# Attention maxima in a two-layer kernel: combining two halves by a pairwise reduce

## The chip, the cores and the metric

The kernel runs on one core of a Trainium2 chip. The metric is the device time of one execution in microseconds, the median of several runs. One further execution was taken by the hardware profiler; its rows are what is called the profile or the trace here. TensorE (PE) does matmuls and transposes, VectorE (DVE), ScalarE (ACT) and GpSimd (POOL) work on elements, and SyncE (SP) issues most transfers. SBUF is the on-chip memory that all engines read; PSUM is the one that TensorE writes.

## The reference

Two layers are computed on an input of 2 x 1024 tokens of width 256. Layer 0 is an attention of 16 query heads on 8 key/value heads of size 16, multiplied by a feed-forward network whose weights are looked up in a table of 16 values. Layer 1 is a recurrence over time, multiplied by a mixture of 8 experts with 2 chosen per token. Only the attention matters for the change:

```python
scores = jnp.einsum('bsdkg,btdk->bkgst', q, k) / jnp.sqrt(jnp.float32(E))
w = jax.nn.softmax(scores, axis=-1)
ctx = jnp.einsum('bkgst,btdk->bkgsd', w, v)
```

The softmax runs over 1024 keys. The kernel subtracts each query's largest score before it takes the exponential, and it is this largest score that the changed line finishes.

## The kernel before

**The work.** A sequence of 1024 tokens and four of its heads (`T`) make a group; there are 2 x 4 = 8 groups. For each group the kernel makes three passes of small matmuls.

- `largest` (letter `m`, L309 and L316) multiplies 128 queries of one head with 512 keys (`mx`, 128x512 in PSUM) and VectorE reduces each row to its maximum, one column of the tile `top`. A block of 128 queries (`c`) needs eight of these: four heads (`i`) times two halves of the keys (`half`). `top` is therefore 128 x 2 x 4: partitions are queries, then the half, then the head. When the eighth is there, L320 takes the larger of the two halves for each head and writes it to slot 16 (`HD`) of the query tile `qn`. That slot meets a constant -1 in the key tile, so that the next product has the maximum subtracted already. Four buffers of `top` rotate.
- `turn_q` with `qTb` (letter `l`, L287) transposes `qn`, now with the maxima, for the second product.
- `weigh` (letter `w`, L340, and L332 in the first group) computes the scores with keys on partitions (`sc`), and ScalarE takes their exponential (`e`, L344). `gather` (letter `v`, L368 and L357) multiplies the exponentials with the values into `cx`; the sum of the weights comes along in a further column. `divide` (letter `y`) divides by it.

The matmuls of `largest` and `weigh` have 32 rows of contraction and take one of four row groups of TensorE each, so four can run side by side. Each writes a bank of its own; there are eight banks, given out in rotation (`bank`), and a matmul waits until the bank's last reader is through: L316 on VectorE for an `mx`, L344 on ScalarE for an `sc`.

**What runs beside it.** GpSimd turns the coded weights of the feed-forward network into numbers (`decode`, letter `z`): for each of 8 pieces and 16 table values it compares the codes with the value's number (L270, 128x544, integers to `pick`) and adds the result to the table of weights (L274, `wlut` plus `pick`, two operands in SBUF). It also rotates queries and keys (L241, L244). The feed-forward network of the tokens that are done (L559, L575) begins within the attention.

**The order.** There is no scheduler: the string `ORDER` is walked letter by letter, and each letter issues the next step of its kind. Every engine executes its instructions in the order in which they were issued, and waits at semaphores for the others. L320 has no letter of its own; it is issued within the step `m` that completes a block, right behind that step's L316, and the next instruction of VectorE is mostly the L316 of the next `mx`.

Of the kernel before, what the change touches and what calls it, by code (L numbers as in the profile page):

```python
# [15 lines left out]
ALU = mybir.AluOpType  # L16
AX = mybir.AxisListType
# [15 lines left out]
HD = 16  # L33
# [69 lines left out]
def attention(  # L103
# [11 lines left out]
    def bank(name):  # L115
        return singles[0].tile([P, 512], F32, tag="one", name=name)
# [18 lines left out]
    qns, kTs, vpf = [], [], []  # L135
# [164 lines left out]
    def largest(n, i):  # L300

        g, u = divmod(n, 16)
        b, T = divmod(g, NQT)
        c, half = divmod(u, 2)
        if (g, c) not in tops:
            tops[g, c] = att2.tile([P, 2, 4], F32, tag="top", name=f"top_{g}_{c}", bufs=4)
        at = slice(SLOT * i, SLOT * (i + 1))
        ps = bank(f"mx_{n}_{i}")
        nc.tensor.matmul(  # L309
            ps,  # L310
            qTs["qTa", g, c // BC][at, ts(c % BC, P)],
            kTs[b][at, T // 2, ts(half, 512)],
            start=True,
            stop=True,
        )
        nc.vector.tensor_reduce(tops[g, c][:, half, i : i + 1], ps, AX.X, ALU.max)  # L316
        done[g, c] = done.get((g, c), 0) + 1
        if done[g, c] == 8:
            top = tops.pop((g, c))
            nc.vector.tensor_tensor(qns[b][:, T, c, :, HD], top[:, 0, :], top[:, 1, :], ALU.max)  # L320

    def weigh(n, i):

# [91 lines left out]
    def each(f, *ranges):  # L415
# [10 lines left out]
        "j": each(turn_q, ["qTa"], range(GROUPS), range(2)),  # L426
        "l": each(turn_first, range(BC)) + each(turn_q, ["qTb"], range(GROUPS), range(2))[1:],
        "m": each(largest, range(UNITS), range(4)),
        "w": each(weigh, range(UNITS), (0, 2, 1, 3)),
        "v": each(gather, range(UNITS)),  # L430
# [1103 lines left out]
```

## Time and profile before

| | |
|---|---|
| median of 3 runs | 979.56 us (979.51 to 980.02) |
| the profiled execution's own time | 980.91 us |
| its span | 979.0 us |
| TensorE clock granted | 0.994 |
| the reduces L316 | 512, 324.7 us, 683 ns each |
| the exponentials L344 | 512, of 605 ns |
| the matmuls `mx` L309 | 1024 records (two for each of 512), 626 ns each |
| the matmuls `sc` L340 | 960 records (two for each of 480), 625 ns each |
| decode L270 to `pick`, L274 | 120 each; 2102 and 1337 ns |
| first and last L320 | 34.1 and 509.1 us |

The span is the time between the first and the last instruction in the profile; the execution's own time contains what lies around it. The page gives busy time by engine, then rows of 40 slices of the span in which a digit is the busy share in tenths, then the chain of work that ended last, followed back from the end, as shares of the span, then groups of instructions by line of the kernel. In a group, `out<-in` names what is written and read, with partitions x elements; after the count come busy time, mean ns of one, and the idle time of the engine just before them with what ended it. The view of waits lists, for an engine and a line, what the wait ended with, its total, how often, and the longest. The timeline gives single instructions, or runs of equal ones, with start and duration in us.

### The profile page before, as it was taken

To read this page: it belongs to the slowest core of one execution; us is meant where nothing else is said; L and a number is where in the kernel's file an instruction comes from. 1 tells how busy PE (TensorE), PEld (TensorE's weight loads), DVE (VectorE), ACT (ScalarE), POOL (GpSimd) and SP (SyncE) were. 2 spreads that over 40 slices of the span, in tenths; PEclk is the share of its full clock that TensorE was granted. 3 is DMA by queue.
4 is the path that set the end of the run, shared out by engine and by line. 5 is a ranking of instruction groups with operands and counts; after the bars stand their busy time and mean duration, and the time that the engine had idled before them with its cause. 6 is when DMAs were issued, how large, how long until landed. Compare 5 with 4: busy or idle time off the path is not lost.

```text
span 979.0 us, 17252 instructions
## 1 busy us (share of the span) xinstructions
PE 953.0 (97%) x6716; PEld 522.4 (53%) x6716; DVE 627.9 (64%) x1228; ACT 533.8 (55%) x1009; POOL 586.7 (60%) x485
## 2 busy tenths in 40 slices
PE   8999999999999999999999999999999999999974
PEld 4685433343333443443435475755457677777763
DVE  5898887887767767765760134466877635721993
ACT  4545856566675675766767545527323544464221
POOL 7999999999999999999902020202002355453243
PEclk9999999999999999999999999999999999999998
DMA  5000000000000000000000031003501122221232
GB/s 175 2 2 13 1 12 1 1 12 1 12 2 1 12 1 13 1 1 1 1 1 1 1 122 40 24 1 101 164 1 33 50 66 63 68 76 50 77 119 87
DMA packets 17864, 34.53 MB, mean 35 GB/s; under 512 B 2893, under 2 KB 11231, under 8 KB 17439
## 3 DMA queue, kind: packets, MB, share of 16 engines
q1 hardware_dynamic: 13527, 21.96, 7.1%
q0 software_dynamic: 3968, 10.80, 3.6%
q8 instruction: 54, 0.88, 0.4%
q10 hardware_dynamic: 288, 0.66, 0.2%
q14 instruction: 27, 0.22, 0.1%
HBM read 22.01 MB, written 11.40 MB: 34 GB/s over the span
## 4 chain that ended last, share of the span: by engine, by line
PE 91%; DVE 5%; issue 1%; DMA 1%; POOL 1%; ACT 0%; POOLq 0%; SPq 0%; ACTq 0%; DVEq 0%
PE sc L340 15%; PE mx L309 14%; PE cx L368 12%; PE gu L559 7%; PE gue L990 5%; PE d L575 4%; PE gus L750 4%; PE dne L1018 3%; PE qkv L218 3%; PE lev L1228 3%; PE sc L332 2%; PE rp L1132 1%; PE so L410 1%; PE vp L1159 1%; PE kp L1132 1%; PE ap L1132 1%
## 5 line engine op out<-in xcount | busy, mean ns | idle before, releaser
L316 DVE TENSOR_REDUCE top<-mx 128x1 f32<-128x512 f32 x512 | 324.7, 683 | 92.7 <-PE mx L309 61.7
L344 ACT ACTIVATE e<-sc 128x512 f32<-128x512 f32 x512 | 271.9, 605 | 139.3 <-PE sc L340 65.4
L309 PE MATMUL mx<-kT,qTa 32*128 32x512 f32 x1024 | 287.0, 626 | 0.4 <-DVE top L316 0.4
L270 POOL TENSOR_SCALAR pick<-idx,lut 128x544 f32<-128x544 int32 x120 | 252.3, 2102 | 11.3
L340 PE MATMUL sc<-qTb,kT 32*128 32x512 f32 x960 | 257.5, 625 | 0.5 <-DVE top L316 0.5
L274 POOL TENSOR_TENSOR wlut<-wlut,pick 128x544 f32<-128x544 f32 x120 | 160.4, 1337 | 10.0
L309 PEld LDWEIGHTS mx<-kT,qTa 32*128 32x128 f32 x1024 | 102.5, 183 | 66.1 <-DVE top L316 27.3
L340 PEld LDWEIGHTS sc<-qTb,kT 32*128 32x128 f32 x960 | 93.2, 183 | 79.3 <-DVE top L316 26.4
L368 PE MATMUL cx<-e,vpad 128*32 128x512 f32 x960 | 123.9, 603 | 0.0
L585 POOL TENSOR_TENSOR sgt<-s_sb,g 128x256 f32<-128x256 f32 x16 | 11.6, 728 | 161.1 <-ACT g L583 161.1
L963 POOL DMA_INDIRECT xg<-xn_h,who x39 | 39.4, 1009 | 94.8 <-PE s L1351 70.2
L1031 POOL DMA_INDIRECT y_h<-ye,who x39 | 39.9, 1024 | 69.2 <-ACT ye L1026 25.4
L559 PE MATMUL gu<-xnT,wlut 128*128 128x512 f32 x160 | 72.8, 597 | 0.0
L368 PEld LDWEIGHTS cx<-e,vpad 128*32 128x32 f32 x960 | 20.8, 108 | 84.2 <-issue 73.5
L1002 DVE TENSOR_TENSOR sge<-sge,gue 128x176 f32<-128x176 f32 x39 | 13.1, 338 | 73.4 <-ACT sge L1001 73.1
L569 DVE TENSOR_TENSOR h<-sg,gu 128x512 f32<-128x512 f32 x20 | 13.8, 688 | 65.4 <-ACT sg L568 50.3
L990 PE MATMUL gue<-wgu,xT 128*128 x156 | 53.0, 462 | 1.6 <-issue 1.0
L559 PEld LDWEIGHTS gu<-xnT,wlut 128*128 128x128 f32 x160 | 29.1, 190 | 34.0 <-issue 29.9
L575 PE MATMUL d<-wlut,h 128*128 128x256 f32 x192 | 44.1, 381 | 0.5 <-ACT s_sb L413 0.5
L750 PE MATMUL gus<-xnT,wgs 128*128 128x512 f32 (+1 forms) x96 | 43.1, 597 | 0.0
L1018 PE MATMUL dne<-wd,hTe 88*128 x156 | 40.0, 380 | 0.5 <-ACT hTe L1011 0.5
L575 PEld LDWEIGHTS d<-wlut,h 128*128 128x128 f32 x192 | 35.7, 190 | 8.1 <-issue 1.8
(235 smaller groups left out, 1346.6 us busy)
## 6 DMA issues: line engine op xcount, KB each, us to landing
xn_h<-xn SPq DMA_DIRECT2D x16, 256.0 KB, 3.4
yk<-y_h SPq DMA_DIRECT2D x16, 256.0 KB, 3.0
wgu<-in_wgu SPq DMA_DIRECT2D x1, 2816.0 KB, 10.9
idx<-in_idx SPq DMA_DIRECT2D x8, 272.0 KB, 2.7
out_x<-g SPq DMA_DIRECT2D x16, 128.0 KB, 1.7
wd<-in_wd SPq DMA_DIRECT2D x1, 1408.0 KB
xs<-in_x SPq DMA_DIRECT2D x2, 512.0 KB, 4.6
w<-in_w SPq DMA_DIRECT2D x1, 1024.0 KB
```

The costliest lines, as they stand in the source:

```text
L270: nc.gpsimd.tensor_scalar(dst, codes[piece], float(j), lut[:, j : j + 1], ALU.is_equal, ALU.mult)
L274: nc.gpsimd.tensor_tensor(wlut[:, at], wlut[:, at], dst, ALU.add)
L309: nc.tensor.matmul(ps, qTs["qTa", g, c // BC][at, ts(c % BC, P)], kTs[b][at, T // 2, ts(half, 512)], start=True, stop=True,)
L316: nc.vector.tensor_reduce(tops[g, c][:, half, i : i + 1], ps, AX.X, ALU.max)
L340: nc.tensor.matmul(ps, kTs[b][at, T // 2, ts(c, P)], qTs["qTb", g, h][at, :], start=True, stop=True)
L344: nc.scalar.activation(e, ps, AF.Exp, scale=1.0 / math.sqrt(E))
L368: nc.tensor.matmul(cxs[g, h][SLOT * i : SLOT * (i + 1), :], values(b, c, 4 * (T // 2) + i), es.pop((n, i)), start=(c == 0), stop=(c == CPB ...
L559: nc.tensor.matmul(hT0[which], wlut[:, lo + kc * P :][:, 0:P], xnT[:, kc, ts(n, 512)], start=(kc == 0), stop=(kc == KC - 1),)
L575: nc.tensor.matmul(po[:, 0:E], hidden(n)[:, f, ts(k, P)], wd0[:, f, :], start=(f == 0), stop=(f == NF0 - 1),)
L750: nc.tensor.matmul(ps[:sz, which, :], wgs[:, kc, which * SH_CH + lo : which * SH_CH + lo + sz], xnT[:, kc, ts(n, 512)], start=(kc == 0), s ...
L990: nc.tensor.matmul(ps[:, 0 : 2 * EI], xT[:, kc, :], late["gu"][:, kc, bass.ds(e * (2 * EI), 2 * EI)], start=(kc == 0), stop=(kc == KC - 1),)
L1018: nc.tensor.matmul(ps[:, 0:E], hT[:, k, :], late["d"][:, k, bass.ds(e * E, E)], start=(k == 0), stop=(k == 1),)
```

## The change

The eight maxima of a block are combined by `tensor_reduce` with `max` over a view of `top` whose innermost dimension is the half: for each of the four heads a pair of values that lie four elements apart. It reads one operand of 128x8 where the operation before read two of 128x4. The result goes to the same four places of `qn`.

```diff
         if done[g, c] == 8:
             top = tops.pop((g, c))
-            nc.vector.tensor_tensor(qns[b][:, T, c, :, HD], top[:, 0, :], top[:, 1, :], ALU.max)
+
+            nc.vector.tensor_reduce(
+                qns[b][:, T, c, :, HD], top.rearrange("p h i -> p i h"), AX.X, ALU.max
+            )
```

## The prediction

> **What bounds the kernel now.** I read the page's totals and chain first, then the groups with their shapes kept apart, then the changed line alone, then the timeline round single executions of it.
>
> ```profile
> PE 953.0 (97%) x6716; PEld 522.4 (53%) x6716; DVE 627.9 (64%) x1228; ACT 533.8 (55%) x1009; POOL 586.7 (60%) x485
> ...
> DVE 5898887887767767765760134466877635721993
> ...
> POOL 7999999999999999999902020202002355453243
> ...
> PE 91%; DVE 5%; issue 1%; DMA 1%; POOL 1%; ACT 0%; POOLq 0%; SPq 0%; ACTq 0%; DVEq 0%
> ```
>
> TensorE is on the chain for 91% of the span, VectorE for 5%. The changed line lies in the attention, the first 515 us (21 slices of 24.5 us); there VectorE is busy 60 to 90% and GpSimd nearly all the time, with the table decode of L270 and L274. So a saving on VectorE counts only where a matmul waits for it. The waits say that this happens:
>
> ```profile
> PEld mx L309 <- DVE top L316: 27.3, 59, 1.0
> PEld sc L340 <- DVE top L316: 26.4, 48, 1.0
> ```
>
> Columns: total us, times, longest. 53.7 us of weight loads wait for the reduce L316 to free a PSUM bank. TensorE hardly looks idle meanwhile, because these matmuls use 32 of 128 rows and four may run side by side: a late one spoils a group of four rather than stopping the engine.
>
> **The changed row** (groups by shape: count, then busy us and mean ns; idle):
>
> ```profile
> L320 DVE TENSOR_TENSOR qn<-top 128x4 f32<-128x4 f32 x64 | 26.0, 407 | 2.2
> ...
> L779 DVE TENSOR_REDUCE top<-left 128x4 f32<-128x32 f32 x4 | 0.7, 186 | 0.1
> ...
> L880 DVE TENSOR_REDUCE pos<-each 128x16 f32<-128x128 f32 x2 | 0.6, 286 | 0.1
> ```
>
> The line alone gives min/median/max of 166/168/1345 ns. A mean of 407 over a median of 168 on four elements is a tail. Listed one by one, 35 of the 64 last 166 to 170 ns (5.8 us together) and 29 are longer (20.2 us together; 15.3 us above 167 ns each). The timeline shows what the long ones share (start us, us):
>
> ```profile
> 454.72 1.33 POOL L274 TENSOR_TENSOR wlut<-wlut,pick 128x544 f32<-128x544 f32 x1
> 454.73 1.34 DVE L320 TENSOR_TENSOR qn<-top 128x4 f32<-128x4 f32 x1
> ```
>
> ```profile
> 107.30 2.10 POOL L270 TENSOR_SCALAR pick<-idx,lut 128x544 f32<-128x544 int32 x1
> 107.53 0.50 DVE L320 TENSOR_TENSOR qn<-top 128x4 f32<-128x4 f32 x1
> ```
>
> In the first pair both end together. Of the 29, 20 were issued behind a running L274 and every one ends 20 to 26 ns after it; they hold 13.0 us of the excess. The other nine came behind a young L270: eight end 729 to 733 ns after its start, one came so early that it ended at 197; 2.3 us. An L320 issued later into an L270 lasts 167 ns. So the operation of two SBUF operands waits while GpSimd reads SBUF.
>
> **Rule and row.** The Trainium skill, "SBUF — State Buffer", section "Who interferes with whom", states that a VectorE instruction with two SBUF inputs contends with a GpSimd instruction that reads SBUF, for the whole instruction, and that tensor_reduce never contends on trn2. "Whole" does not fit L270: the row is let go after 0.73 of 2.10 us. By the rule a random L320 would wait (2.10² + 1.34²)/(2 × 3.6) = 0.86 us in each L270/L274 period of about 3.6 us, 55 us over 64; measured are 15.3. I use 15.3. For the rule's other half there is a row, a one-input read of SBUF inside L274:
>
> ```profile
> 31.10 0.18 DVE L170 BATCH_NORM_AGGREGATE mv_a<-bst_a 128x2 f32<-128x6 f32 x1
> ```
>
> ```profile
> 30.92 1.33 POOL L274 TENSOR_TENSOR wlut<-wlut,pick 128x544 f32<-128x544 f32 x1
> ```
>
> With 1.15 us of L274 still to run it takes 0.18, like all 16 of its kind (181 to 184 ns). A rule against the change: "VectorE: DVE Perf Modes", section "Rules for kernel authors", calls tensor_reduce the slowest VectorE operation, to be expected at one element per cycle, and advises restructuring. By it, eight elements instead of four pairs cost four elements more: at L880 minus L779, (286 − 186)/96 = 1.04 ns each, 64 × 4 = 0.3 us. The rows decide below.
>
> **The change part by part.**
> - *Removed*: 64 L320 rows, 26.0 us of VectorE.
> - *Added*: 64 reduces 128x4<-128x8, in the same places with the same wait (on the last reduce into top). No row has this shape. The line through L779 and L880 gives 186 − 24 × 1.04 = 161 ns; L316 (512 elements, 683 ns, from PSUM) lies on it too (152.7 + 1.04 × 512 = 685), so outputs as such cost nothing visible. Bounds: 150 ns (just under the shortest small rows, such as the reciprocal L179 at 155) and 207 ns (L779 plus a further 21 for runs of two elements at a stride, which no row shows). I take 161. Sum: 10.3 us.
> - *VectorE*: 26.0 − 10.3 = 15.7 us less, of which 15.3 are waits for GpSimd.
> - *Moved*: nothing. In the built programs all engines keep their order and only these 64 rows differ. GpSimd's decode keeps its 430 us; the tightest matmul that reads a decoded table (L575, at 521 us) has 32 us in hand, so it does not become the bound.
>
> **How much of 15.7 reaches the end.** I carried the shorter rows forward through the orders and semaphore waits of the built program: each instruction starts after the latest of its predecessor, its producers and, on TensorE, the freeing of its row group, with the gap that the trace shows behind that latest one. A saving dies where VectorE then waits for a matmul, and lives where a matmul was held for a bank. Two cases of it:
>
> ```profile
> 367.46 0.90 DVE L320 TENSOR_TENSOR qn<-top 128x4 f32<-128x4 f32 x1
> ...
> 369.02 0.18 PEld L309 LDWEIGHTS mx<-kT,qTa 32*128 32x128 f32 x1 [0.98 <-DVE top L316]
> ```
>
> Here the loads stand 0.98 us behind the delayed reduces, and 0.74 us of the stall is paid. At 454.73 the 1.18 us of stall are free: TensorE's next mx comes at 458.97, behind cx (456.06) and gu (457.06), and VectorE is through by 457.9. Over the 64 rows it gives, by the row's time in us: 0.54 (74), 0.16 (85), 0.92 (129), 0.55 (137), 0.05 (145), 0.25 (200), 0.79 (210), 0.21 (245), 0.01 (318), 0.87 (327), 0.80 (335), 0.16 (362), 0.74 (367), 0.69 (437), 0.20 (466): 6.9 us, and 7.0 with the 6 ns saved in each row. At 150 ns a row it is 7.1, at 207 ns 6.3. What is late next is the exp on ScalarE (sc and mx loads wait 34.7 us for it within the attention) and TensorE itself; the carry contains both. Everything after 515 us moves up unchanged.
>
> From the profiled execution's own 980.91 us (span 979.0 and 1.9 round it): 974.0. The median of the runs is 979.56, 1.35 below that execution, so the forecast is 979.56 − 6.9 = **972.7 us**.
>
> **The rivals** (times against the median; 0.2%, 2 us, is about what can be told from no change).
> - *Hidden*: TensorE is the bound and VectorE idles 92.7 us before L316, so the gap takes the saving. For: 91% of the chain. Against: the 53.7 us of loads. The chain itself holds three stalled L320 rows (327.49, 367.46, 437.03: excess 0.86 + 0.74 + 0.76 = 2.4 us). If those alone count: 977.2. If ScalarE stands close behind in these too, or the reduce stalls as L320 does: 979 to 980, no change.
> - *More*: the carry keeps every gap, but gaps also shrink when groups of four fill again. At most all 15.7: 963.9. Likely not beyond 10 to 11.
> - *Slower*: the reduce asks for the shared port too and waits out each whole GpSimd instruction, 0.86 + 0.16, about 1.05 us, at each of the 64 places. Carried forward, such rows add 25 us: 1004.8. Spread evenly over all places a cost breaks even at about 0.46 us a row; above that the kernel is slower. For: GpSimd is busy 95 of 100 us there. Against: L170 above, and L316, never over 693 ns in 512 executions.
>
> **How the numbers follow.** Gain of 4.5 to 9 us (970.5 to 975): 0.70. More: 0.06. Between 2 and 4.5: 0.10. Within 2: 0.09. Slower: 0.05. So faster 0.86, same 0.09, slower 0.05. The range 969.0 to 977.5 takes in the carry's bounds, the chain's 2.4 and gains up to 10.5; outside it are the no-change and slower cases and the largest gains, under 0.2.
>
> **What would show it.** The new row x64 at about 161 ns mean with none above 200; VectorE busy near 612 us; loads' waits for L316 below 53.7 us; the last L316 (508.4 us before) near 501.5; the span after it unchanged in length. I am wrong if the new row has a tail that ends with L274, if its mean is above 0.2 us, or if it is short and the last L316 does not come earlier.

## The result and the profile after

The changed kernel takes 974.61 us (median of 5 runs, 972.66 to 975.35) against 979.74 before (5 runs, 979.51 to 982.18). The ratio is 0.9933 with a 95% interval of 0.9917 to 0.9950: faster, by 6.6 us on 980. The medians alone are 5.1 us apart; the clock, at the end of this section, tells why. The forecast was 972.7 in a range of 969.0 to 977.5.

These are the page's totals and chain of the changed kernel (span 973.6 us, own time 975.35):

```profile
PE 948.9 (97%) x6716; PEld 522.3 (54%) x6716; DVE 613.6 (63%) x1228; ACT 533.7 (55%) x1009; POOL 586.9 (60%) x485
...
DVE  5898886877767666665750134476866725621993
...
PE 93%; DVE 4%; issue 1%; POOL 1%; ACT 0%; POOLq 0%; ACTq 0%; DVEq 0%
```

VectorE was busy for 627.9 us before and is for 613.6 now; ScalarE and GpSimd are as they were. VectorE's share of the chain has gone from 5% to 4%, TensorE's from 91% to 93%.

L316 in the groups of VectorE by shape before, the groups now, then the changed line alone (min/median/max in ns, first and last start):

```profile
L316 DVE TENSOR_REDUCE top<-mx 128x1 f32<-128x512 f32 x512 | 324.7, 683 | 92.7 <-PE mx L309 61.7 <-PE sc L340 27.8 <-PE sc L332 0.7
```

```profile
L316 DVE TENSOR_REDUCE top<-mx 128x1 f32<-128x512 f32 x512 | 325.9, 684 | 100.1 <-PE mx L309 66.1 <-PE sc L343 31.1 <-PE sc L335 0.2
...
L321 DVE TENSOR_REDUCE qn<-top 128x4 f32<-128x8 f32 x64 | 10.5, 164 | 2.2
```

```profile
L321 DVE TENSOR_REDUCE qn<-top x64: 162/164/168, 34.3 to 502.4; 128x4 f32<-128x8 f32 x64
```

The tail up to 1345 ns is gone: no row lasts more than 168 ns. 17 of the 64 start in an L274 that has more than 0.3 us to run, and none of them waits. One of these is the same row of the program as the long one at 454.73 before (timelines of VectorE and of GpSimd):

```profile
447.60 0.69 DVE L316 TENSOR_REDUCE top<-mx 128x1 f32<-128x512 f32 x1 [1.39 <-PE mx L309]
448.33 0.16 DVE L321 TENSOR_REDUCE qn<-top 128x4 f32<-128x8 f32 x1
449.54 0.69 DVE L316 TENSOR_REDUCE top<-mx 128x1 f32<-128x512 f32 x1 [1.05 <-PE sc L343]
```

```profile
448.25 1.34 POOL L274 TENSOR_TENSOR wlut<-wlut,pick 128x544 f32<-128x544 f32 x1
```

It is also one where the saving is worth nothing: VectorE then stands idle for 1.05 us until the next product. Where it was worth something, the loads no longer stand so long behind L316 (waits within the attention, 20 to 515 us):

```profile
PEld sc L343 <- DVE top L316: 24.4, 46, 0.8
PEld mx L309 <- DVE top L316: 23.7, 51, 0.8
```

48.1 us instead of 53.7. **The attention** is best read from the first to the last L316, before and after (min/median/max in ns, first and last start):

```profile
L316 DVE TENSOR_REDUCE top<-mx x512: 671/682/693, 27.7 to 508.4; 128x1 f32<-128x512 f32 x171
```

```profile
L316 DVE TENSOR_REDUCE top<-mx x512: 672/681/694, 28.0 to 501.7; 128x1 f32<-128x512 f32 x171
```

That is 480.7 us before and 473.7 now: 7.0 us shorter. The rest of the program follows 6.7 us earlier (it began 0.3 later), and that holds to within 0.05 us until 942 us of the span. Then 1.2 us are given back while the granted clock is lower. The stretch from 940 to 950 us, before and after (busy us and count by engine, granted TensorE clock, DMA share, GB/s):

```profile
940.00:950.00 10.00, 6.28 (x44) 4.79 (x40) 9.78 (x18) 3.14 (x7) 4.71 (x6) 0.88 0.57 167
```

```profile
940.00:950.00 10.00, 9.75 (x58) 8.00 (x60) 7.73 (x15) 4.11 (x8) 3.95 (x5) 0.69 0.25 74
```

The second program is 6.7 us further on in its row, so the busy times are not those of the same work. The clocks (0.88 and 0.69) are what counts: here the granted clock falls to half for 3.4 us before (947.7 to 951.1) and for 6.8 us after (939.4 to 946.3). Runs of one kernel mostly fall in two groups: before, in all comparisons but the last, 979.3 to 980.4 us with a mean clock of 0.994 to 0.996 and 981.7 to 982.2 with 0.993 (two executions, at 980.9 and 981.1, lie between); after, 972.7 and 973.1 with 0.995, and 974.6 to 975.4 with 0.993. Within either group the kernels are about 7 us apart; three of the five runs after lie in the group at 0.993 and one of the five before, which is why the medians differ by less.

### The profile page after: what moved, and what is told of

It reads as the page before. It is cut to its first block, busy times and chain, and to the rows that moved or that the text cites. A ratio compares the mean times of both kernels' runs of the same rounds, so it can differ in the third digit from the quotient of the medians.

```text
span 973.6 us, 17252 instructions
## 1 busy us (share of the span) xinstructions
PE 948.9 (97%) x6716; PEld 522.3 (54%) x6716; DVE 613.6 (63%) x1228; ACT 533.7 (55%) x1009; POOL 586.9 (60%) x485
## 4 chain that ended last, share of the span: by engine, by line
PE 93%; DVE 4%; issue 1%; POOL 1%; ACT 0%; POOLq 0%; ACTq 0%; DVEq 0%
PE sc L343 15%; PE mx L309 14%; PE cx L371 12%; PE gu L562 7%; PE gue L993 5%; PE d L578 4%; PE gus L753 4%; PE dne L1021 3%; PE qkv L218 3%; PE lev L1231 3%; PE sc L335 2%; PE so L413 2%; PE vp L1162 1%; PE rp L1135 1%; PE kp L1135 1%; PE ap L1135 1%
## 5 line engine op out<-in xcount | busy, mean ns | idle before, releaser
L316 DVE TENSOR_REDUCE top<-mx 128x1 f32<-128x512 f32 x512 | 325.9, 684 | 100.1 <-PE mx L309 66.1
L309 PE MATMUL mx<-kT,qTa 32*128 32x512 f32 x1024 | 282.8, 625 | 0.3 <-DVE top L316 0.3
L270 POOL TENSOR_SCALAR pick<-idx,lut 128x544 f32<-128x544 int32 x120 | 252.5, 2105 | 11.3
L343 PE MATMUL sc<-qTb,kT 32*128 32x512 f32 x960 | 254.8, 624 | 0.0
L274 POOL TENSOR_TENSOR wlut<-wlut,pick 128x544 f32<-128x544 f32 x120 | 160.7, 1339 | 10.0
```

The costliest lines, as they stand in the source:

```text
L270: nc.gpsimd.tensor_scalar(dst, codes[piece], float(j), lut[:, j : j + 1], ALU.is_equal, ALU.mult)
L274: nc.gpsimd.tensor_tensor(wlut[:, at], wlut[:, at], dst, ALU.add)
L309: nc.tensor.matmul(ps, qTs["qTa", g, c // BC][at, ts(c % BC, P)], kTs[b][at, T // 2, ts(half, 512)], start=True, stop=True,)
L343: nc.tensor.matmul(ps, kTs[b][at, T // 2, ts(c, P)], qTs["qTb", g, h][at, :], start=True, stop=True)
```

## The experiments

Times are medians; "attention" is the length from first to last L316 in the profile (480.7 us before, 473.7 changed). Where two variants lie close together, runs with the same mean clock are compared.

**Is it GpSimd's decode?** In two kernels GpSimd fills each piece of the table with zeros instead of decoding it; layer 0's feed-forward network then computes with zero weights. One has the operation of two operands, one the reduce.

```diff
-        if j:
-            dst = att2.tile([P, LSTEP], F32, tag="pick", ...)
-        nc.gpsimd.tensor_scalar(dst, codes[piece], float(j), lut[:, j : j + 1], ...)
-        if j:
-            nc.gpsimd.tensor_tensor(wlut[:, at], wlut[:, at], dst, ALU.add)
+        if j == 0:
+            nc.gpsimd.memset(dst, 0.0)
```

> The operation of two operands as before, but GpSimd decodes no weights: each piece of the table of weights is filled with zeros by one memset, so that L270 and L274 are gone and layer 0's feed-forward network computes with zero weights (that part of the result is left out). Theory of the shared read (VectorE's operation of two SBUF operands waits for GpSimd's reads): all 64 L320 rows shrink to 166 to 170 ns, except a few beside the short rotations L241 and L244; total near 10.8 us instead of 26.0; the time falls by about 7 us to 971 to 974, the same as for the reduce without decode within 1 us. Rival (the operation of two operands is slow for its own operands, such as a bank clash inside top): the rows keep their tail and the time stays near 979.5.

> The pairwise reduce with the decode left out as in tt_quiet (zero weights in layer 0's feed-forward network). Theory of the shared read: nothing is left for it to gain, rows 162 to 168 ns and a time of 971 to 974.5, within 1 us of tt_quiet, so that the change is worth 7 us with the decode and nothing without it. Rival (the reduce is the cheaper operation for its own sake): still 5 to 7 us below tt_quiet, near 967.

Measured: 972.66 us for the two operands (ratio to before 0.9924, 0.9910 to 0.9938) and 972.77 for the reduce (0.9929, 0.9914 to 0.9943); attention 473.6 and 473.5. The attention and the old operation in the quiet kernel with two operands, the latter also in the groups by shape:

```profile
L311 DVE TENSOR_REDUCE top<-mx x512: 672/682/694, 26.8 to 500.4; 128x1 f32<-128x512 f32 x171
```

```profile
L315 DVE TENSOR_TENSOR qn<-top 128x4 f32<-128x4 f32 x64 | 10.7, 167 | 2.2
```

```profile
L315 DVE TENSOR_TENSOR qn<-top x64: 166/167/169, 33.1 to 501.1; 128x4 f32<-128x4 f32 x64
```

Not one of 64 rows is long, though nothing about the operation or its operands was changed. With the decode the change is worth 7 us, without it nothing. The tail comes from GpSimd's decode; and taking that work away altogether brings the attention no further than the reduce does (473.5 to 473.7), so the reduce removes all of this cost. Leaving the decode out takes away its reads and its writes together. One row bears on which of them counts: at 206.29 the old operation starts 0.5 us into a memset of GpSimd, which writes and reads nothing, and lasts 166 ns. So the writing did not hold it there, but this is a single row.

**The wait in the queue, or the wait of the readers?** Behind each reduce a second operation on the same `top` goes to a tile that nobody reads, once the old one (first cut) and once the reduce (second cut).

```diff
+            nc.vector.tensor_tensor(spare, top[:, 0, :], top[:, 1, :], ALU.max)
```

```diff
+            nc.vector.tensor_reduce(spare, top.rearrange("p h i -> p i h"), AX.X, ALU.max)
```

> The changed kernel, with the old operation of two operands issued behind each reduce into a spare tile that nothing reads: nobody waits for its result, it only stands in VectorE's queue. Theory of the shared read: its 64 rows have the old tail (mean 350 to 420 ns, long ones ending with L274 or 0.73 us after the start of L270), and carried forward through the changed kernel's trace they cost 9.8 us: about 984, slower than before. Rival (only the row's own length counts, and the wait lay on the result's readers): the spare rows cost what the spare reduces of reduce_plus_reduce cost, about 2.3 us: 977.

> The changed kernel, with the same reduce issued a second time into a spare tile that nothing reads. It prices 64 more rows of about 164 ns (about 105 ns of queue each, since rows overlap by some 60 ns) without any wait: carried forward 2.3 us, so 976 to 978. Rival (VectorE's queue has room everywhere, and only waits of the readers count): no change, 974.6.

Measured: 980.36 us with the spare operation of two operands (ratio to before 1.0000, 0.9992 to 1.0008), attention 480.8: the gain is wholly lost, 7.1 us, with the reduce in place and no reader for the spare result:

```profile
L317 DVE TENSOR_REDUCE top<-mx x512: 671/682/694, 27.3 to 508.1; 128x1 f32<-128x512 f32 x171
```

With the spare reduce 974.69 (0.9941, 0.9928 to 0.9954), attention 475.0. That the second median equals the changed kernel's is an accident of the clock groups; at 0.994 and 0.995 its runs are 974.5 to 975.1 against 972.7 and 973.1, so that 64 more rows cost 1.3 (attention) to 1.8 us. The two spare rows by shape:

```profile
L325 DVE TENSOR_TENSOR spare<-top 128x4 f32<-128x4 f32 x64 | 22.8, 357 | 0.0
```

```profile
L325 DVE TENSOR_REDUCE spare<-top 128x4 f32<-128x8 f32 x64 | 9.7, 152 | 0.0
```

Same place, same input, same absence of readers, 152 against 357 ns. 25 of the two-operand rows exceed 200 ns; all end either 17 to 23 ns after an L274 or 726 to 729 ns after the start of an L270 (here L275 and L271). One of the former, with the L275 beside it:

```profile
200.21 1.19 DVE L325 TENSOR_TENSOR spare<-top 128x4 f32<-128x4 f32 x1
```

```profile
200.04 1.34 POOL L275 TENSOR_TENSOR wlut<-wlut,pick 128x544 f32<-128x544 f32 x1
```

Both end at about 201.4. So the price lies in VectorE's queue: what stands behind the blocked operation, the L316 that free banks, comes late. The expected sizes were too large: 9.8 forecast and 7.1 measured, 2.3 forecast and 1.3 to 1.8 measured.

**Long single stalls, or VectorE's time as such?** A spare reduce of 128x144 elements spreads about the same time evenly over the 64 places.

```diff
+            nc.vector.tensor_reduce(
+                spare, kTs[b][:, 0, 0:144].rearrange("p (i s) -> p i s", i=4), AX.X, ALU.max
+            )
```

> The changed kernel with a spare reduce behind each of the 64, 128x4<-128x144 from the key tile in SBUF, which nothing reads: about 300 ns each, about 225 ns of queue, 14 us in all, near the 12 to 15 us that the two-operand rows lose, but spread evenly and without waiting for GpSimd. If VectorE's time counts wherever it falls, it costs what the stalls cost, 5 to 7 us over the changed kernel: 978 to 980 at a clock of 0.995. If evenly spread time is taken up by VectorE's gaps and only the long single stalls reach the matmuls: 1 to 3 us, 974 to 976.

Measured: 977.67 us (0.9977, 0.9962 to 0.9991); rows of 293 ns. The runs with a clock of 0.995 are at 976.9 to 977.9, about 4.5 us above the changed kernel's 972.9. (In its profile the clock was also halved for 6.8 us from 66.3. Outside the 12 us around that, its L316 fall 3.8 us behind those of the changed kernel.) That is between the two theories.

What share of VectorE's time reaches the end can be counted, with the time from a row's start to that of VectorE's next instruction, at most 50 ns past the row's end. The even spare rows take 14.4 us of queue, and 3.8 to 4.5 of it, 26 to 31%, reach the end. The spare reduces take 5.5 us, of which 1.3 to 1.8, or 24 to 33%, count. The spare rows of two operands take 18.4 us, of which 7.1, or 39%, count. For the changed line the same count gives 21.6 us before and 6.4 now, a difference of 15.2 us, of which 7.0, or 46%, reached the end. So evenly spread time counts too, only somewhat less than long single stalls.

**Fewer rows.** The transposes need the maxima of four blocks anyway, so one operation can serve four blocks (except in the first four, which are transposed singly): 19 rows for 64, of 128x16. Once with the reduce, once with two operands.

```diff
-            tops[g, c] = att2.tile([P, 2, 4], F32, tag="top", ..., bufs=4)
+            tops[m] = att2.tile([P, BC, 2, 4], F32, tag="top", ..., bufs=2)
...
-        if done[g, c] == 8:
+        if done[m] == 8 * k:
...
+            nc.vector.tensor_reduce(to, top.rearrange("p c h i -> p c i h"), AX.X, ALU.max)
```

> The changed kernel with one pairwise reduce for four blocks of queries (128x16<-128x32, about 186 ns) instead of one a block, the first four blocks apart: 19 rows instead of 64, since the transposes wait for four blocks anyway. If 45 rows of queue (70 to 80 ns each, 3.4 us) count at the rate of the carry, 0.7 us faster than the changed kernel: 972 in runs with a clock of 0.995, 974 at 0.993. Rival, from reduce_plus_reduce, where 64 more short rows cost nearly nothing: no difference that can be seen, 972.7 and 974.8.

> The same batching with the operation of two operands (128x16 from two of 128x16): 19 rows that may wait for GpSimd instead of 64. Theory of the shared read: about 29 of 64 still wait in proportion, so 6 to 11 long rows and 3 to 6 us of excess instead of 15.3, costing 1 to 3 us over reduce_by_four: 973 to 976. Rival (number of rows does not matter, the operation itself does): near 979.5 as before.

Measured: 972.79 us for the reduce (0.9921, 0.9908 to 0.9935), attention 472.5, 1.2 less than the changed kernel, but a time that cannot be told from the changed kernel's 972.7 and 973.1; 973.52 for two operands (0.9931, 0.9917 to 0.9946), attention 474.0. The latter's line alone shows the tail again, on fewer rows:

```profile
L326 DVE TENSOR_TENSOR qn<-top x19: 166/189/1358, 33.6 to 501.9; 128x16 f32<-128x16 f32 x15, 128x4 f32<-128x4 f32 x4
```

Five rows are long, all behind an L274, with 3.8 us of excess; the attention is 1.5 us longer than with the batched reduce. Batching alone takes 6.7 of the 7.0 us that the change takes, since it leaves fewer chances to meet GpSimd.

**Another operation that waits.** The normalisations L199 (SBUF to SBUF on VectorE, 397 to 1409 ns) go to ScalarE. (Four small VectorE operations that negate a mean, not in the cut below, come in for them.)

```diff
-        if t < CPB:
-            nc.scalar.activation(xn, xs[:, t, :], AF.Identity, bias=mvs[t], scale=rstds[t])
-        else:
-            nc.vector.tensor_scalar(xn, xs[:, t, :], mvs[t], rstds[t], ALU.subtract, ALU.mult)
+        nc.scalar.activation(xn, xs[:, t, :], AF.Identity, bias=mvs[t], scale=rstds[t])
```

> The changed kernel with the eight normalisations L199 of the second sequence (tensor_scalar from SBUF to SBUF on VectorE, 397 to 1409 ns, the long ones beside GpSimd's L270 and L274) moved to ScalarE, as those of the first sequence are. If they wait for the same shared port, VectorE loses 2 us of waits and 3 us of work; carried forward 0.4 us faster, 972.3 at a clock of 0.995. Rival: ScalarE's 0.6 us each delay the exponentials as much: no difference or 0.5 us slower.

Measured: 972.53 us (0.9924, 0.9910 to 0.9940), attention 473.6; at 0.995 its runs are 972.3 to 972.5 against 972.7 and 973.1. The sign is as forecast, but a difference of 0.1 in the attention cannot be told from none.

**Side by side.** The changed kernel, the batched one, and both last edits together, in turn on one chip:

> The changed kernel once more, so that it and the two versions below are timed on one chip in turn. Its five earlier runs fell in two groups, 972.7 to 973.1 at a mean granted clock of 0.995 and 974.6 to 975.4 at 0.993; the kernel before has 979.3 to 980.4 at 0.994 to 0.996 and 981.7 to 982.2 at 0.993. If the change is worth 6.9 us in either group, the same two groups again.

> One reduce for four blocks (reduce_by_four) once more. Its attention ended 1.2 us earlier than the changed kernel's, counted from first to last reduce of a bank. If that counts, 0.7 to 1.5 us below reduce_again at the same clock; if the tail takes it, equal to it.

> One reduce for four blocks and the normalisations of the second sequence on ScalarE, together. The latter alone ended the attention 0.1 us earlier than the changed kernel. Expected within 0.5 us of by_four_again.

This chip was slower in the expert stage (before: 995.06 us). The changed kernel took 987.99 (0.9931, 0.9917 to 0.9946), the batched one 986.57 (0.9915, 0.9902 to 0.9928), both edits 986.44 (0.9917, 0.9905 to 0.9930). The expected two clock groups did not show there, since the clocks spread from 0.986 to 0.993. The attention was 473.6, 472.4 and 472.2 us. The batched reduce is the best version found, by 1.4 us in the medians and 1.2 in the attention, though its runs and those of the changed kernel overlap a little (985.3 to 987.1 and 986.4 to 990.3); what the second edit adds to it cannot be told from nothing.

## Why the prediction was right

- *The tail and its cause.* Held. The excess of 15.3 us belonged to GpSimd's decode: it is gone with the reduce, gone for the old operation when the decode is gone, and back when the old operation is added behind the reduce. That it is the decode's reading, as the prediction has it, rests on the rule it cites and on the one row beside a memset.
- *The rule on the shared port and the row.* Of the rule cited from the Trainium skill, "SBUF — State Buffer", section "Who interferes with whom", the half on tensor_reduce held in this case: 64 rows and 64 spare ones, none above 168 ns. The half that says "for the whole instruction" did not: the spare rows behind the same GpSimd operation (L271 there) were again let go early, 726 to 729 ns after its start, with about 1.4 us of it to run. The rule against the reduce, one element per cycle, cost nothing that can be seen on eight elements.
- *The new row.* 161 ns was taken from the line through two other reduces; measured 164. Two values at a stride cost nothing noticeable.
- *VectorE.* 15.7 us less busy were expected and 14.3 came; the changed rows alone gave 15.5 (26.0 to 10.5). The rest is no slower work: the page counts time in which two rows overlap once, and with more gaps between them (idle before L316 100.1 us, 92.7 before) the L316 overlap less. Their busy time rose from 324.7 to 325.9 us while one takes 684 ns in place of 683.
- *How much reaches the end.* 7.0 us by the carry and 7.0 in the attention, and not in the total alone. Counted from the first L316, the changed kernel was ahead by 0.66 us at 100 us, 2.17 at 160, 3.58 at 300, 5.25 at 360, 6.68 at 440 and 6.96 at the last L316; the prediction's list adds up to 0.70, 2.22, 3.47, 5.15, 6.74 and 6.94 at these places. So the mechanism held stretch by stretch, though between these places the difference strays from the list by up to some 0.8 us. That it held to 0.1 us is more than the method can promise: the same carry forecast 9.8 for the spare pair and got 7.1, and 2.3 for the spare reduce and got 1.3 to 1.8. It keeps every gap as it was, and real gaps may give a little. For removing time it was right, for adding time roughly a third or more too high.
- *The end.* "The span after it unchanged in length" held up to 942 us and then failed by 1.2 us, for the clock. That, with the 0.3 us before the first L316, makes up the 1.4 us between the forecast of 974.0 for the profiled execution and its 975.35. The median lies 1.9 us above its forecast because three of its five runs are in the group at 0.993; those at 0.995 (972.7 and 973.1) lie at the forecast. The prediction put the clock at nothing.
- *The rivals.* The chain's own three stalled rows, 2.4 us, were far too little to count by. The gain stayed well below the 15.7 us of the third case. The slower case, a reduce that asks for the port too, was ruled out by the first view of the new row.

## What to carry to other kernels

A mean far above the median in a tiny VectorE operation points to a wait: list its rows one by one against GpSimd's timeline, and see whether they end together. If the operation reads two operands from SBUF while GpSimd reads, one operand in a single view can do the same work at the same length without the wait; fewer and larger such operations help nearly as much. What it brings is the part of the stall behind which TensorE waits for a bank, here about half of it, and the chain's own entries for the line understate it.

## What the runs showed of the hardware

A VectorE operation of 4 elements with two SBUF operands was held until 17 to 26 ns after the end of a GpSimd tensor_tensor of 128x544, but only until 726 to 733 ns after the start of a GpSimd tensor_scalar of the same size that lasts 2.10 us. Why the second lets go at a third of its length was not tested. The batched form, with 16 elements per operand, ended 42 to 46 ns after the tensor_tensor. The pairwise reduce was held by neither.

In all 13 profiles TensorE stands idle for 3.1 us, waiting for VectorE, some 35 us before the end, and the granted clock is at half at the very end. In 12 of them it also falls to half near that idle stretch: for 6.8 us in the four where it fell 0.5 to 1.0 us before TensorE resumed (the changed kernel's is one), for 3.4 us in the eight where it fell between 0.2 us before that moment and 1.6 us after it (the profile before is one). In reduce_plus_pair it did not fall there. Behind the last L316, on the chips other than that of the last comparison, the program took 469.8 us without such a fall, 470.6 to 471.0 with the short one and 471.9 to 472.3 with the long one: about 1 us for each 3.4. That is about half of what parts the two groups. The first L316 also starts anywhere from 26.7 to 28.0 us; the cause of that stays open.

The Trainium skill, "TensorE: Matmul & The Clock Gate", section "What's actually happening", states that an idle window of about 3.4 us halves the clock, and that these windows run on their own and do not start anew with the kernel. The lengths agree with one and two windows, and where the fall came against the idle stretch goes with its length, as it would if the windows' phase decided. But the 3.4 us ahead of these falls were not wholly idle: 0.3 to 1.6 us of TensorE work lay in them. No run set the phase.
